# Unread products in TensorE's two pauses of the last stage of a two-layer gated transformer

## The chip, the cores and the metric

The kernel runs on one core of one Trainium2 chip. The metric is the device time of one launch in microseconds. The other engines of the core are named as in the profile: PE is TensorE's matmul, PEld its weight load, DVE is VectorE, ACT is ScalarE, POOL is GpSimd and SP is SyncE.

## The reference

The input x has 8 batches of 256 tokens of 256 features, and ctx has the same shape. Two layers follow each other. Each adds a gated attention and a gated feed-forward part to x:

```python
x = x + tanh(g_xattn[0]) * L0_xattn(layernorm(x), ctx)      # 16 heads of 16
x = x + tanh(g_ffn[0])   * L0_ffn(layernorm(x))             # 64 slots, top 8, a GRU
x = x + tanh(g_xattn[1]) * L1_xattn(ctx, layernorm(x))      # 8 heads of 128
x = x + tanh(g_ffn[1])   * L1_ffn(layernorm(x))
```

The change lies in the last of these four. L1_ffn works on values that are rounded to 8-bit steps:

```python
def _act_fake_quant(x, clip_factor):
    scale = sigmoid(clip_factor) * max(abs(x)) / 127.0       # over the whole tensor
    return clip(round(x / scale), -128, 127) * scale

xq   = _act_fake_quant(x, clip_x)
gate = xq @ quant(w_gate).T          # 256 -> 704
up   = xq @ quant(w_up).T
h    = _act_fake_quant(silu(gate) * up, clip_down)
out  = h @ quant(w_down).T           # 704 -> 256
```

What matters here is that each scale is one maximum over all tokens. No up product can start before the maximum of the whole normed x is known, and no down product before the maximum of the whole h is known. So TensorE has two pauses in this stage.

## The kernel before, in words

Layers 0 and 1 are worked through batch by batch in one long, interleaved run. In `attention1` the loop is over 8 batches of 8 heads, and the pieces of layer 0 for later batches stand in a queue `side` with a cost for each and due times; they are drawn in between the steps of layer 1. When the last batch begins, the queue has been emptied, and `ffn_weights` adds the quantizing and turning of the weights w_gate, w_up and w_down to it. The results are wgT, wuT and wdT, bf16 tiles with 128 partitions. wdT has six blocks of 256 columns.

The last batch ends with `project(0)` and `project(1)` (line 1092, 8 heads each, fp32), then `norm` (the layer norm xl, line 245, and the largest value of the batch, amax, line 1122), then `turn_x` (four transposes of xl, line 254, copied by ACT at line 1129).

The last stage then goes:

1. `act_scale` (lines 1350 to 1363) for x. DVE takes the maximum over the columns of amax (1353), PE transposes the column into a row (1355), DVE takes the maximum of the row (1356), PE spreads the one number over 128 partitions with a product of ones (1358), and DVE makes the scale sx (1360) and its reciprocal rx (1362).
2. `quantize_tokens` (1383) for each batch: a scaling to int8 (1370 on ACT, 1372 on DVE) and a cast to bf16 (1373). The result is xqT.
3. `expand` (1387) for each of four groups of 512 tokens. In each, six tiles of the 704 middle features follow: four products of 128x512 bf16 into a PSUM tile `big` of which there are three (1394), Silu on ACT into sg (1402), and the multiplication into h, on DVE (1409) or for every third tile on ACT and POOL (1406, 1407). `largest` (1427) collects the maxima of h on DVE into hmax.
4. `act_scale` again for h: sh and rh.
5. For each batch, h is scaled and cast to bf16 hq (1370, 1372, 1373), twelve products of 128x256 bf16 go into a PSUM tile `one` (1459), DVE multiplies with the scales into y (1467), POOL adds x (1469, on DVE for the last batch), and SP stores y (1470).

The tiles `one` (two buffers) serve both `act_scale` and the down products. Before the pools `big` and `one` are opened, PSUM is held by the pools of `bank`: four buffers "m", three "z" and one "s".

The order on each engine is set by a scheduler that follows the order in which the kernel was written, except where an instruction is ready sooner. `tc.issue_after(ins)` queues what is written in its block behind `ins` on the same engine; it adds an order and no wait for `ins` to finish.

## Time and profile before

| | us |
|---|---|
| median of 3 timed runs | 1047.76 |
| lowest and highest of them | 1046.73, 1048.28 |
| the profiled execution | 1043.28 |
| its span, first to last instruction | 1041.5 |
| PE busy | 990.5 (95%) |
| DVE busy | 623.7 (60%) |
| ACT busy | 463.9 (45%) |
| POOL busy | 121.5 (12%) |
| mean granted clock of PE | 0.975 |

The stage that the change touches is the last 70 us of the span. It can be read from the timeline:

| from the span's start, us | what |
|---|---|
| 970.87 to 974.59 | the second output projection (1092) on PE |
| 974.59 to 978.17 | PE pauses |
| 978.17 to 980.76 | four transposes of xl, and the two small steps of the first scale on PE |
| 980.76 to 983.14 | PE pauses |
| 983.14 to 1010.88 | up products (1394) |
| 1010.88 to 1014.62 | PE pauses |
| 1014.62 to 1015.94 | the two small steps of the second scale |
| 1015.94 to 1018.35 | PE pauses |
| 1018.35 to 1036.75 | down products (1459) |
| 1038.27 | DVE's last instruction; the last store follows |

The profile gives each engine's busy time by slices and, in the row PEclk, the share of full speed that the clock of the PE array was granted. Views by window give the same numbers for any stretch. In the timeline an instruction's row ends with the idle time of its engine ahead of it and who ended it.

### The profile page before, as it was taken

The page shows a single profiled execution, that of the slowest core. Times are in us where ns is not written, and L with a number is a line of the kernel's source. Part 1 is how long each engine was busy: PE and PEld are TensorE (multiplying, and loading weights), DVE is VectorE, ACT ScalarE, POOL GpSimd, SP SyncE. Part 2 cuts the span into 40 slices and gives each one's busy share as a digit, 9 for nine tenths or more (in the row PEclk, how much of TensorE's full clock was granted, in tenths as well). Part 3 has the DMA queues.
Part 4 walks back from the last instruction along what each step waited for, and adds up shares of the span by engine and source line. Part 5 has one row for each costly group of instructions (what it writes and reads, how often), then busy time and mean ns, then how long its engine had stood idle before and what let it go on. Part 6 is the DMA issues. An engine that isn't in the chain of part 4 may idle for free.

```text
span 1041.5 us, 13065 instructions
## 1 busy us (share of the span) xinstructions
PE 990.5 (95%) x4803; PEld 683.5 (66%) x4803; DVE 623.7 (60%) x1613; ACT 463.9 (45%) x878; POOL 121.5 (12%) x158
## 2 busy tenths in 40 slices
PE   5998799999999999999999999999999999999776
PEld 4765466667677667777776676676776776776423
DVE  5655566656465655756566564566765365454397
ACT  3666335444435533444534434444334234234474
POOL 5201120101010010111001000010000000000134
PEclk9989889999999999999999999999999999999897
DMA  7702200021110101111000100001000000000002
GB/s 172 200 1 72 91 21 21 28 74 41 52 50 22 51 31 41 36 46 41 21 21 31 51 21 21 29 1 56 1 1 1 1 0 1 1 1 1 1 0 82
DMA packets 33536, 37.32 MB, mean 36 GB/s; under 512 B 10368, under 2 KB 28992, under 8 KB 33472
## 3 DMA queue, kind: packets, MB, share of 16 engines
q1 hardware_dynamic: 33472, 36.48, 11.9%
q8 instruction: 38, 0.62, 0.2%
q14 instruction: 26, 0.21, 0.1%
HBM read 28.08 MB, written 8.39 MB: 35 GB/s over the span
## 4 chain that ended last, share of the span: by engine, by line
PE 87%; DVE 7%; ACT 2%; DMA 2%; issue 1%; POOL 1%; SPq 0%; DVEq 0%; ACTq 0%; POOLq 0%
PE bank_m L1020 11%; PE bank_m L1051 11%; PE bank_m L1079 10%; PE bank_m L1033 10%; PE bank_m L1005 6%; PE bank_m L1065 5%; PE bank_m L1092 5%; PE bank_z L598 4%; PE bank_z L635 3%; PE bank_z L622 3%; PE bank_z L506 2%; PE bank_z L535 1%; PE bank_s L845 1%; PE bank_z L671 1%; PE bank_m L254 1%; PE bank_m L635 1%
## 5 line engine op out<-in xcount | busy, mean ns | idle before, releaser
L1053 ACT ACTIVATE e<-bank_m,nm 128x512 f32<-128x512 f32 x128 | 88.0, 688 | 146.2 <-DVE nm L1052 144.0
L1051 PE MATMUL bank_m<-k,q 128*128 128x512 f32 x256 | 127.3, 602 | 0.0
L1020 PE MATMUL bank_m<-kvT,w1kv 128*128 128x512 f32 x256 | 126.1, 604 | 0.0
L1079 PE MATMUL bank_m<-eT,v 128*128 128x256 f32 x512 | 124.8, 381 | 1.1 <-ACT e L1053 0.7
L1079 PEld LDWEIGHTS bank_m<-eT,v 128*128 128x128 f32 x512 | 95.3, 190 | 34.4 <-issue 16.3
L1033 PE MATMUL bank_m<-w1kv,kvT 128*128 128x256 f32 x512 | 116.6, 380 | 0.0
L1052 DVE TENSOR_REDUCE nm<-bank_m 128x1 f32<-128x512 f32 x128 | 87.9, 688 | 33.7 <-PE bank_m L1051 32.9
L1033 PEld LDWEIGHTS bank_m<-w1kv,kvT 128*128 128x128 f32 x512 | 95.9, 190 | 13.7 <-issue 1.1
L625 ACT ACTIVATE e<-bank_z 128x512 f32<-128x512 f32 x112 | 63.2, 596 | 80.9 <-PE bank_z L622 80.7
L240 POOL TENSOR_TENSOR rstd<-rstd,mhalf 128x2 f32<-128x2 f32 x48 | 34.7, 726 | 446.6 <-DVE rstd L239 410.1
L1014 DVE TENSOR_SCALAR q<-bank_m,bq 128x256 f32<-128x256 f32 x64 | 28.1, 479 | 97.1 <-PE bank_m L1005 97.0
L601 DVE TENSOR_REDUCE nf<-bank_z 128x2 f32<-128x512 f32 x112 | 75.0, 683 | 18.0 <-PE bank_z L598 17.6
L1040 DVE COPY v<-bank_m 128x512 f32<-128x512 f32 x64 | 43.9, 686 | 58.0 <-PE bank_m L1033 58.0
L1065 PEld LDWEIGHTS bank_m<-ident,e 128*128 128x128 f32 x512 | 58.5, 140 | 23.4 <-issue 18.2
L1065 PE MATMUL bank_m<-ident,e 128*128 128x128 f32 x512 | 71.4, 275 | 0.4 <-DVE v L1040 0.4
L1022 ACT ACTIVATE k<-bank_m,bk 128x512 f32<-128x512 f32 x64 | 44.0, 688 | 55.2 <-PE bank_m L1020 55.1
L1086 ACT ACTIVATE oT<-bank_m,bv 128x256 f32<-128x256 f32 x64 | 30.3, 474 | 84.4 <-PE bank_m L1079 84.1
L1005 PE MATMUL bank_m<-kvT,w1q 128*128 128x256 f32 x256 | 64.1, 388 | 1.3 <-DVE kvT L991 1.0
L1055 DVE TENSOR_SCALAR e<-e,rs 128x512 f32<-128x512 f32 x128 | 62.1, 485 | 2.2
L1051 PEld LDWEIGHTS bank_m<-k,q 128*128 128x128 f32 x256 | 44.5, 190 | 26.6 <-issue 22.0
L1020 PEld LDWEIGHTS bank_m<-kvT,w1kv 128*128 128x128 f32 x256 | 43.0, 190 | 28.1 <-issue 24.6
L1092 PE MATMUL bank_m<-w1o,oT 128*128 128x256 f32 x256 | 59.6, 380 | 0.6 <-DVE x L1106 0.6
(345 smaller groups left out, 1547.8 us busy)
## 6 DMA issues: line engine op xcount, KB each, us to landing
qs<-dqb SPq DMA_DIRECT2D x96, 64.0 KB, 2.5
ks<-dkb SPq DMA_DIRECT2D x48, 128.0 KB, 2.7
c<-in_ctx_dram SPq DMA_DIRECT2D x8, 256.0 KB, 3.2
x<-in_x_dram SPq DMA_DIRECT2D x8, 256.0 KB, 2.9
w1kv<-in_L_xattn_Wkv_dram SPq DMA_DIRECT2D x4, 512.0 KB, 6.8
out_dram<-y SPq DMA_DIRECT2D x8, 256.0 KB, 2.1
dqb<-hi SPq DMA_DIRECT2D x6, 256.0 KB, 2.1
dqb<-lo SPq DMA_DIRECT2D x6, 256.0 KB, 2.4
```

Of the source, the lines that this page charges most:

```text
L601: V.tensor_reduce(full[:, 2 * half : 2 * half + 2], ps, AX.X, ALU.max, negate=True)
L625: A.activation(e[:, i, :, :], ps, AF.Exp)
L1005: T.matmul(pq[:, i, :], w1q[:, c, h * P : (h + 1) * P], self.kvT[:, c, S:], start=c == 0, stop=c == 1,)
L1020: T.matmul(pk, w1kv[:, c, h * P : (h + 1) * P], self.kvT[:, c, :], start=c == 0, stop=c == 1)
L1033: T.matmul(pv[:, k, :], self.kvT[:, c, kc * P : (kc + 1) * P], w1kv[:, c, at : at + 2 * P], start=c == 0, stop=c == 1,)
L1051: T.matmul(ps, self.q[h][:, qc * P : (qc + 1) * P], self.k[h], start=True, stop=True)
L1052: V.tensor_reduce(nm[:, at], ps, AX.X, ALU.max, negate=True)
L1053: A.activation(e[:, qc, :], ps, AF.Exp, bias=nm[:, at], accum_out=sums[:, at])
L1055: V.tensor_scalar(e[:, qc, :], e[:, qc, :], rs[:, at], None, ALU.mult)
L1065: T.transpose(pt[:, k, qc * P : (qc + 1) * P], self.e[h][:, qc, kc * P : (kc + 1) * P], ident)
L1079: T.matmul(po, self.v[h // 2][:, kc, (h % 2) * P : (h % 2 + 1) * P], self.eT[:, kc, :], start=kc == 0, stop=kc == 3,)
L1092: T.matmul(self.pp[:, qc, :], self.oT[:, h, qc * P : (qc + 1) * P], w1o[:, h, :], start=h == 0, stop=h == H1 - 1,)
```

## The change

A function `keep_busy(to, n)` makes n products of wdT with itself: the first 128 columns are the weights, the first 512 columns are moved through, and the result goes into a PSUM tile that nobody reads. It is called in four places, with 14, 8, 15 and 9 products: behind the second output projection of the last batch, behind the broadcast of the first scale, behind the last up product, and behind the broadcast of the second scale. `project` and `expand` now hand on their last matmul, so that the calls can be queued behind it.

```diff
+WARM = (14, 8, 15, 9)
...
-                T.matmul(
+                self.projected = T.matmul(
                     self.pp[:, qc, :],
                     self.oT[:, h, qc * P : (qc + 1) * P],
                     w1o[:, h, :],
                     start=h == 0,
                     stop=h == H1 - 1,
-                )
+                ).ins
...
+    def keep_busy(to, n):
+
+        w = ffn["wdT"].rearrange("p i d -> p (i d)")[:, :512]
+        for _ in range(n):
+            T.matmul(to, w[:, :P], w, start=True, stop=True)
...
         me.project(0)
         me.project(1)
+        with tc.issue_after(me.projected):
+            keep_busy(bank("s"), WARM[0])
         me.norm()
         me.turn_x()
...
-        def act_scale(maxima, clip_col, name):
+        def act_scale(maxima, clip_col, name, after):
...
-            T.matmul(pb[:, 0:1], ones[:1, :], m[:1, 1:2], start=True, stop=True)
+            bc = T.matmul(pb[:, 0:1], ones[:1, :], m[:1, 1:2], start=True, stop=True)
+            with tc.issue_after(bc.ins):
+                keep_busy(one(), after)
...
-        sx, rx = act_scale(amax, clip[:, 0:1], "x")
+        sx, rx = act_scale(amax, clip[:, 0:1], "x", WARM[1])
...
-        expand(NB - 1)
+        filled = expand(NB - 1)
         while hold:
             largest()
 
-        sh, rh = act_scale(hmax, clip[:, 1:2], "h")
+        with tc.issue_after(filled):
+            keep_busy(one(), WARM[2])
+        sh, rh = act_scale(hmax, clip[:, 1:2], "h", WARM[3])
```

Nothing that the reference asks for is left out or computed in another way.

More of the change, by code (lines that the diff above doesn't have):

```diff
@@ L1393, in expand @@
                     for c in range(2):
-                        T.matmul(
+                        ins = T.matmul(
                             pg[:m, w, :],
@@ L1399, in expand @@
                             stop=c == 1,
-                        )
+                        ).ins
                 sg = fp.tile([P, 512], F32, tag="sg", name="sg", bufs=3)
@@ L1420, in expand @@
                     hold.append((3 * n + 2, n, 5 if last else 3, 6))
+            return ins
         hold = []
```

## The prediction

> **What bounds the kernel now.** I read the slices first. TensorE (PE) is busy nearly everywhere, but its busy share falls in the last three slices, and there the granted clock falls too.

> ```profile
> PE   5998799999999999999999999999999999999776
> ...
> PEclk9989889999999999999999999999999999999897
> ```

> So I asked for the busy time in windows. The clock changes at 976.80, 987.04, 1014.35 and 1024.59 us; the distances 10.24, 27.31 and 10.24 are 3, 8 and 3 times 3.413, so I cut on that grid. After the stretch come its length, then busy us (instructions) of PE, PEld, DVE, ACT and POOL, then the granted clock, DMA share and GB/s. The first two rows are from early in the kernel.

> ```profile
> 27.89:31.31 3.42, 2.21 (x15) 1.46 (x14) 3.34 (x11) 1.18 (x3) 0.34 (x1) 1.00 0.76 249
> 92.75:96.16 3.41, 2.21 (x15) 1.76 (x16) 2.59 (x7) 2.49 (x5) 1.91 (x3) 1.00 0.81 200
> 973.39:976.80 3.41, 1.20 (x6) 0.72 (x4) 1.70 (x6) 0.00 (x0) 0.29 (x1) 1.00 0.00 0
> 976.80:980.21 3.41, 1.60 (x6) 0.83 (x6) 1.75 (x7) 0.58 (x1) 2.13 (x5) 0.50 0.00 0
> 983.63:987.04 3.41, 3.41 (x10) 1.21 (x9) 0.00 (x0) 2.76 (x6) 0.65 (x1) 0.50 0.00 0
> 987.04:990.45 3.41, 3.41 (x17) 1.30 (x15) 2.53 (x3) 2.78 (x6) 0.98 (x2) 1.00 0.02 5
> 1010.93:1014.35 3.42, 0.00 (x0) 0.00 (x0) 3.42 (x5) 0.68 (x1) 0.27 (x1) 1.00 0.00 0
> 1014.35:1017.76 3.41, 0.95 (x3) 0.57 (x3) 2.17 (x9) 1.33 (x2) 0.00 (x0) 0.50 0.00 0
> 1017.76:1021.17 3.41, 2.38 (x10) 1.02 (x11) 3.25 (x5) 3.41 (x4) 0.00 (x0) 0.50 0.00 0
> 1021.17:1024.59 3.42, 3.42 (x15) 1.45 (x13) 1.56 (x2) 3.42 (x3) 1.73 (x1) 0.50 0.01 2
> 1028.00:1031.41 3.41, 2.30 (x16) 1.28 (x15) 3.41 (x5) 1.47 (x1) 2.26 (x2) 1.00 0.23 82
> ```

> The reader is to see: after a window with PE busy 1.20 (973.39) or 0.00 (1010.93) the clock halves; it comes back only after a window that is full (983.63, 1021.17); 2.38 busy at half clock (1017.76) did not bring it back. Busy 2.30 at full clock (1028.00) kept it. With 2.21 it was once lost (27.89) and once kept (92.75). I put the bound for keeping near 2.2 of 3.41.

> The timeline shows what the half clock costs.

> ```profile
> 983.14 1.01 PE L1394 MATMUL big<-xqT,wgT 128*128 128x512 bf16 x2 [2.38 <-ACT xqT L1373]
> ...
> 987.64 0.59 PE L1394 MATMUL big<-xqT,wgT 128*128 128x512 bf16 x2
> ...
> 988.76 0.69 ACT L1402 ACTIVATE sg<-big,cg 128x512 f32<-128x512 f32 x1 [0.23 <-PE big L1394]
> ...
> 1022.09 0.69 DVE L1467 TENSOR_TENSOR y<-one,srow 128x512 f32<-128x512 f32 x1 [1.08 <-PE one L1459]
> ...
> 1024.98 0.69 DVE L1467 TENSOR_TENSOR y<-one,srow 128x512 f32<-128x512 f32 x1 [1.33 <-PE one L1459]
> ```

> Two up products take 0.85 us at half clock (starts 984.80 and 985.65) and 0.43 at full (987.64 and 988.07). ScalarE waits for PE before each of its first sg, and VectorE waits 1.08 and 1.33 us for the down products. The chain of waits agrees: 4.68 us of PE at L1394 from 983.14 and 5.34 us of PE at L1459 from 1019.61 end last. Between them VectorE is the bound: from 993.55 to 1014.40 it has no pause over about 0.1 us.

> [...]

> **The change, part by part.** The instruction order shows only PE changed: 46 products with their weight loads. The 14 stand behind the last output projection, 8 behind the first scale's broadcast, 15 behind the last up product, 9 behind the second scale's broadcast. None of them carries a wait. No DMA, ACT, DVE or POOL instruction is moved.

> *The added products.* At full clock one costs 0.216 us: 128x512 bf16, as L1394 at 987.64. What stands behind them on PE waits for other engines anyway:
> - 14 x 0.216 = 3.02 us; PE is idle 3.58 us there (974.59 to 978.17, waiting for xl).
> - 8 x 0.216 = 1.73; idle 2.38 (980.76 to 983.14, for xqT).
> - 15 x 0.216 = 3.24; idle 3.73 (1010.89 to 1014.62, for mh).
> - 9 x 0.216 = 1.94; idle 2.41 (1015.94 to 1018.35, for hq).

> The least slack is 0.47, so I cost them at nothing. At half clock they are 5.98, 3.42, 6.40 and 3.84 and overshoot by 2.4, 1.0, 2.7 and 1.4: that is the price if the cover is gone.

> *The added waits.* PE waits for its own earlier products at the second scale's transpose and before batch 1's down products (WAW on a `one` bank): long done, nothing. Three more allocations turn the two `one` banks: batch 0's down product takes the bank that sh reads at 1015.98, free 2 us before 1018.35. Nothing.

> *First gap.* With the clock held, the three transposes from 978.71 to L1355 (0.67 us) take half, -0.34. L1355 at 0.42 comes near the 0.27 of L611's full-clock median, -0.1; L1358 at 0.58 near 0.42 (L367: 0.17 to 0.25 each), -0.15. So xqT and all behind it come 0.6 earlier. PE then starts up products at 982.5, and a tile of four takes 0.86 instead of 1.71. Tile 0 is ready at 983.6, before ScalarE has done its casts (984.83 - 0.6 = 984.2). From there ScalarE runs back to back at about 0.6 each: sg0 984.2, up0 984.8, sg1 985.4, sg2 986.0, sg3 986.6 instead of 988.76, 2.2 earlier. VectorE: h1 at 986.1 instead of 987.47, h2 986.8, the first hmax 987.65 instead of 989.42: 1.8 earlier. What is late next is VectorE itself; h4 stands behind hmax, so the 1.8 goes on to 1014.4.
> Will the clock hold? PE is busy until 977.65, then only about 1.0 to 1.3 us until the 8 start at 980.1. The worst window, 977.65 to 981.06, has 1.6 to 2.1: under my bound. So it may fall between about 979.8 and 981.7. Then up to 8 products run at 0.43 and the up products start near 983.6 instead of 982.5, but the window is full and the clock is back by then or one window later: tile 0 at 984.6, gain 1.4. Ends: 0.6 (clock back late) and 2.2. I take 1.8.

> *Second gap.* L1355 and L1358 cost -0.2. The worst windows hold about 2.0 to 2.4 busy, at the bound or over it. With the clock held, down products start-to-start are 0.145 us (12 in 1.78, at 1029.13) instead of 0.25. Batch 0's last nine, from 1019.57, are done at 1021.05: y0 at 1021.1 instead of 1022.09, -1.0. Batch 1's twelve follow until 1022.65: y1 at 1022.8 instead of 1024.98, -2.15. Behind it VectorE is continuous to 1035.6, and what it needs from ScalarE is there (the cast of batch 3 ends at 1023.87, before qh of batch 6 would start at 1024.3), so -2.15 reaches the end; the last PE wait of 1.25 us stays, since that batch waits for y5's bank. Ends: 0 (clock lost) and 2.6 (both waits and the small steps); I take 2.15 + 0.2 = 2.3.

> **Sum.** 1.8 + 2.3 = 4.1 us against the profiled execution: 1043.28 us, of which 1041.5 is span. The median of the timed runs, 1047.76, lies 4.48 above it; I take the difference over. [...] So 4.4: 1047.76 - 4.4 = 1043.4 us.

> **The rivals.**
> - One gap only. The window around the short groups of down products has about 2.0 busy and may lose the clock. For: 2.21 lost it once. Against: 2.30 kept it. Then 1.8 + 0.3 remain, about 1045.6.
> - Full clock, but ScalarE takes over. It is busy 4.79 to 5.00 us of each 5 from 990 to 1000; if its queue does not start earlier, the first gap is worth 0.6 only: 1047.76 - 0.6 - 2.3 = 1044.9. Against: its waits before sg name PE.
> - It doesn't do what it says: the products don't keep the clock, or it falls in the same places; delay and earlier return cancel: 1047.8.
> - Slower. The products run at half clock and stand in front of the real ones. Place: PE's queue at 974.6, 980.8, 1010.9 and 1015.9; price up to 7.5 us, with nothing gained: 1055.3. It decides if the clock is already down, or falls, while one of the longer groups runs: a product at half clock takes 0.21 more, so more than two of the 15 (slack 0.49) already hold up mh. Against: the windows before both gaps are busy 2.84 and 2.95 and at full clock.

> **How the numbers follow.** Forecast 0.60, own range 1041.6 to 1044.9; one gap 0.17; ScalarE 0.10; no effect 0.08; slower 0.05. The range reaches over the first three to 1046.0 and leaves the last two and the ends out. About 0.2%, 2.1 us, can be told from no change. Faster by more: 0.60 + half of 0.17 + 0.09 = 0.78; within: 0.17; slower: 0.05.

> **What would show it.** In the changed profile: PE clock 1.00 in the windows from 983 to 988 and from 1015 to 1024, or a short dip near 980; up products 0.43 for two from the first tile; the first sg not waiting for PE; the waits of 1.08 and 1.33 us before y gone; the added products ended before xl, xqT, mh and hq arrive. Wrong if the last stage keeps a half clock behind 1018, if L254 or L1355 wait for the added products, or if the first hmax is less than 1 us earlier relative to the last projection.

## The result and the profile after

The changed kernel takes 1040.92 us in the median of 9 runs (1038.1 to 1043.36), the kernel before 1046.73 in the median of 9 (1043.22 to 1050.4). The medians lie 5.8 us apart. The recorded ratio of the two kernels, which I go by, is 0.9958 with a 95% interval of 0.9943 to 0.9974: 4.4 us less, between 2.7 and 6.0. The profiled execution has a span of 1040.2 us.

The slices of the profile, in the same two rows as before: the last three slices are now at full clock.

```profile
PE   5999899999999999999999999999999999999886
...
PEclk9988889999999999999999999999999999999999
```

The view by windows on the clock's grid; columns as in the prediction. In this trace too the clock changes on a grid of 3.413 us: its half-clock spells ahead of the stage last 10.24, 10.24, 6.83 and 6.83 us. The grid stands at another place than in the profile before.

```profile
976.03:979.45 3.42, 3.42 (x18) 2.00 (x17) 1.70 (x6) 0.00 (x0) 0.13 (x1) 1.00 0.00 0
979.45:982.86 3.41, 2.26 (x13) 1.06 (x11) 1.75 (x7) 0.58 (x1) 2.48 (x5) 1.00 0.00 0
982.86:986.27 3.41, 2.86 (x14) 1.26 (x14) 1.89 (x7) 2.86 (x5) 0.41 (x2) 1.00 0.03 7
1010.17:1013.58 3.41, 3.41 (x17) 1.30 (x15) 3.31 (x5) 1.79 (x3) 1.30 (x1) 1.00 0.00 0
1013.58:1016.99 3.41, 2.55 (x13) 1.12 (x12) 2.38 (x6) 0.00 (x1) 0.00 (x0) 1.00 0.00 0
1016.99:1020.41 3.42, 2.30 (x13) 0.81 (x10) 3.42 (x6) 3.42 (x4) 0.00 (x0) 1.00 0.02 5
```

Every window is granted the full clock. The two weakest hold 2.26 and 2.30 us of PE work, just over the 2.21 behind which the clock was once lost and once kept in the kernel before. No other place of the grid would have been weaker by more than 0.01: slid over the two pauses, a stretch of 3.41 us holds at least 2.26 and 2.29 us of PE work.

The timeline after, on DVE, ACT, PE and POOL. The line numbers are those of the changed file: 1251 the added products, 1406 the up products, 1414 sg, 1474 the down products, 1482 y.

```profile
977.24 3.19 PE L1251 MATMUL bank_s<-wdT 128*128 128x512 bf16 x14
...
985.30 0.59 PE L1406 MATMUL big<-xqT,wgT 128*128 128x512 bf16 x2 [0.55 <-ACT xqT L1385]
...
986.90 0.68 ACT L1414 ACTIVATE sg<-big,cg 128x512 f32<-128x512 f32 x1
...
989.55 0.69 ACT L1414 ACTIVATE sg<-big,cg 128x512 f32<-128x512 f32 x1 [0.25 <-POOL h L1419]
...
1021.67 0.69 DVE L1482 TENSOR_TENSOR y<-one,srow 128x512 f32<-128x512 f32 x1
...
1022.44 3.85 POOL L1484 TENSOR_TENSOR y<-y,x 128x512 f32<-128x512 f32 x2 [10.48 <-DVE y L1482]
...
1023.40 0.69 DVE L1482 TENSOR_TENSOR y<-one,srow 128x512 f32<-128x512 f32 x1 [0.17 <-PE one L1474]
1024.01 1.16 DVE L1385 CAST hq<-qh 128x1536 bf16<-128x1536 int8 x1
```

The up products start at full speed (starts 985.30 and 985.73, 0.43 us for two). The first sg no longer waits for PE; the fourth (989.55) waits for POOL instead. Of the two waits of 1.08 and 1.33 us before y, 0.17 is left.

To compare profiles I count from one event, the start of VectorE's second update of x by the last projection (974.63 in the profile before, 977.45 after), because the time up to there differs between profiles of equal code by up to 5 us. "mh" is the start of the reduction behind the last hmax, "end" the end of VectorE's last instruction. In us:

| kernel | first hmax | mh | mh to end | whole stage | ratio to before (95%) |
|---|---|---|---|---|---|
| before | 14.79 | 39.77 | 23.87 | 63.64 | |
| after | 12.82 | 37.72 | 21.75 | 59.47 | 0.9958 (0.9943 to 0.9974) |
| again | 12.82 | 37.72 | 21.74 | 59.46 | 0.9942 (0.9925 to 0.9959) |
| gap1 | 12.82 | 37.75 | 23.25 | 61.00 | 0.9982 (0.9959 to 1.0005) |
| gap2 | 14.82 | 39.78 | 21.66 | 61.44 | 0.9968 (0.9956 to 0.9981) |
| thin | 14.79 | 39.77 | 23.87 | 63.64 | 0.9989 (0.9976 to 1.0003) |
| half | 12.84 | 37.77 | 23.09 | 60.86 | 0.9973 (0.9946 to 1.0000) |
| over | 13.88 | 38.24 | 23.05 | 61.29 | 0.9965 (0.9951 to 0.9979) |
| short_only | 13.70 | 38.63 | 21.84 | 60.47 | 0.9970 (0.9954 to 0.9985) |
| long_only | 14.47 | 39.44 | 23.68 | 63.12 | 0.9985 (0.9970 to 1.0000) |
| rows32 | 14.85 | 39.82 | 24.84 | 64.66 | 1.0020 (1.0005 to 1.0036) |
| cols32 | 12.82 | 37.74 | 21.76 | 59.50 | 0.9946 (0.9931 to 0.9962) |
| early1 | 12.82 | 37.42 | 21.77 | 59.19 | 0.9952 (0.9937 to 0.9968) |
| early2 | 12.83 | 37.75 | 21.74 | 59.49 | 0.9952 (0.9937 to 0.9968) |

The stage is 4.17 us shorter: 2.05 up to mh, 2.12 behind it.

### The profile page after: what moved, and what is told of

Its sections match the earlier page's. It is cut to its first block, busy times and chain, and to the rows that moved or that the text cites. A ratio compares the mean times of both kernels' runs of the same rounds, so it can differ in the third digit from the quotient of the medians.

```text
span 1040.2 us, 13158 instructions
## 1 busy us (share of the span) xinstructions
PE 999.1 (96%) x4849; PEld 688.4 (66%) x4849; DVE 624.2 (60%) x1613; ACT 463.0 (45%) x878; POOL 121.1 (12%) x158
## 4 chain that ended last, share of the span: by engine, by line
PE 87%; DVE 7%; ACT 3%; issue 1%; POOL 1%; DMA 1%; SPq 0%; DVEq 0%; ACTq 0%; POOLq 0%
PE bank_m L1022 11%; PE bank_m L1053 11%; PE bank_m L1081 10%; PE bank_m L1035 10%; PE bank_m L1007 6%; PE bank_m L1067 5%; PE bank_m L1094 5%; PE bank_z L600 4%; PE bank_z L624 3%; PE bank_z L637 3%; PE bank_z L508 3%; PE bank_z L537 1%; PE bank_s L847 1%; PE bank_z L673 1%; PE bank_m L256 1%; PE bank_m L637 1%
```

## The experiments

My theory: the products keep PE busy enough in each window that the clock stays, and that alone makes the real products of this stage faster. Rivals: the changed order or turn of the PSUM tiles made the gain; only both pauses together pay; any busy PE will do; the products themselves delay the real work.

### Each pause alone: gap1 and gap2

```diff
-WARM = (14, 8, 15, 9)
+WARM = (14, 8, 0, 0)      # gap1
+WARM = (0, 0, 15, 9)      # gap2
```

A call with no products is left out, with its tile.

> Only the first two groups (14 and 8 products). If the gain is the held clock in each pause by itself: from the last batch's second update of x to the start of the reduction mh 37.7 us as after the change (39.8 before), from there to VectorE's last instruction 23.2 as before; 2.0 us faster than before, ratio about 0.998. If the gain came from the second pause alone: no change. If the added work only pays in both together: under 1 us.

> Only the last two groups (15 and 9 products). If each pause pays by itself: 39.8 us from the second update of x to mh as before, 21.1 from there to VectorE's end (23.2 before); about 2.1 us faster, ratio about 0.998. If the second pause holds the clock only when the first did: no change.

(These two, and the two runs behind them, count the stage to the start of VectorE's last instruction; the table counts to its end, 0.69 us later.)

gap1 reached mh at 37.75 and gap2 needed 21.66 behind it: each pause pays by itself, with the sizes expected. The two gains do not wait for each other. One number is off: gap1's second half, with no products in it, took 23.25 instead of 23.87. In gap1 the clock fell 1.5 us before mh and was back 8.75 us behind it, in the kernel before it fell with mh and was back 10.2 us behind it. The whole first half is 2.0 us earlier against the grid, so the half clock meets another part of the work; this explanation was not tested by itself. The ratios agree with this, but gap1's interval reaches 1.

### The same places without work: thin

```diff
-            T.matmul(to, w[:, :P], w, start=True, stop=True)
+            T.matmul(to[:32, :1], w[:, :32], w[:, :1], start=True, stop=True)
```

> All 46 products, in the same places and into the same tiles, but with 32 columns of weights and 1 column moved, so that they keep PE busy for a small part of the time. If the clock is what counts: it halves in both pauses, 63.0 us from the second update of x to VectorE's end as before, ratio 1.000. If the changed order or the other turn of the PSUM tiles brought the gain: 58.8 us, ratio 0.996. The results of the real computation are not changed.

PE's timeline of this kernel: the first group now is over in half a microsecond, and the four transposes behind it take 1.42 us again, as at half clock in the kernel before (0.30 and 0.55 us after the change).

```profile
976.27 0.50 PE L1251 MATMUL bank_s<-wdT 128*32 128x1 bf16 x14
979.92 1.42 PE L256 MATMUL bank_m<-ident,xl 128*128 128x128 f32 x4 [3.15 <-DVE amax L1124]
```

Every mark of the stage is that of the kernel before to 0.01 us. Order, waits and tiles are those of the changed kernel, so these bring nothing; the gain comes from the work that PE does there (stage 63.64 us without it, 59.47 with it).

### Once more: again

No edit; the changed kernel.

> The changed kernel once more, to see it at another place of the clock's windows. If the products hold the clock at any place: 58.8 us from the second update of x to VectorE's end, within 0.5, and ratio 0.996. If they hold it only at some places: a half clock at about 980 or 1019 in this profile, and up to 2 us longer.

59.46 us. The clock held with the grid 0.9 us later against the stage than in the first profile. early2 below, with the same pauses, has the grid 1.6 us later than the first profile, and its stage takes 59.49.

### Fewer products: half

```diff
-WARM = (14, 8, 15, 9)
+WARM = (7, 4, 8, 5)
```

> Half of the products: 7, 4, 8 and 5. The stretches between groups grow by 1.5, 0.9, 1.5 and 0.9 us. If a window keeps the clock only from about 2.2 us busy on, it falls in both pauses: first hmax about 14.2 us after the second update of x (12.8 with all products, 14.8 with none), whole stage about 62.5 us (59.5 and 63.6). If a little activity is enough: 59.5.

The windows of this kernel at both pauses:

```profile
977.49:980.90 3.41, 1.41 (x8) 0.91 (x9) 1.78 (x8) 0.59 (x1) 2.49 (x5) 1.00 0.00 0
980.90:984.32 3.42, 2.75 (x7) 0.81 (x6) 1.85 (x7) 3.00 (x6) 0.28 (x2) 0.50 0.02 7
1011.62:1015.04 3.42, 1.23 (x6) 0.68 (x7) 2.39 (x7) 0.10 (x1) 0.00 (x0) 1.00 0.00 0
1015.04:1018.45 3.41, 2.21 (x8) 0.56 (x6) 3.41 (x6) 3.41 (x4) 0.00 (x0) 0.50 0.00 0
```

The clock fell in both pauses, behind windows with 1.41 and 1.23, as expected. But 2.75 in one window was enough to bring it back at 984.32, so the first hmax came at 12.84, not at 14.2, and the stage at 60.86, not at 62.5: my expectation took a wholly busy window as the condition, and that was wrong. The first pause could do with half of the products, at this place of the grid. In the second pause 2.21 did not bring it back, and of the 2.12 us only 0.78 are left.

### Too many products: over

```diff
-WARM = (14, 8, 15, 9)
+WARM = (22, 14, 24, 15)
```

> More than fits: 22, 14, 24 and 15 products, at 0.216 us 4.75, 3.02, 5.18 and 3.24 us for pauses of 3.58, 2.38, 3.73 and 2.41. The clock holds, and the overshoot stands on the path: the transposes of xl 1.2 later, the up products 1.0 to 1.6 later in all, the transpose of mh another 1.45, the last group nothing or 0.1, since ScalarE's half of batch 0 comes later. Stage about 62 to 62.6 us instead of 59.5. If PE's queue let the real work go ahead of the products: 59.5.

PE's timeline of this kernel at the first pause:

```profile
974.59 4.70 PE L1251 MATMUL bank_s<-wdT 128*128 128x512 bf16 x21
979.12 0.60 PE L256 MATMUL bank_m<-ident,xl 128*128 128x128 f32 x4
```

(One of the 22 products has no record here.) The transposes start 4.55 us behind the update of x instead of 3.54: they wait for the products. The stage takes 61.29 us, a little less than the 62 to 62.6 expected. The up products were 1.1 us later and the first hmax still 1.06, but mh only 0.5: ScalarE did a cast (0.5 us) ahead of its first sg that in the changed kernel stands behind its fourth, and VectorE has one wait of 0.42 less before mh. Behind mh 1.30 was lost, where the estimate was 1.45. So the price of the products that did not fit was here the overshoot, less what the engines behind made up again.

### One group of each pair: short_only and long_only

```diff
-WARM = (14, 8, 15, 9)
+WARM = (0, 8, 0, 9)       # short_only
+WARM = (14, 0, 15, 0)     # long_only
```

> Only the short groups (8 and 9), behind each scale's broadcast. The clock is lost in the long pauses, and the short groups run at half speed, 3.4 and 3.8 us, past the end of their pauses by about 1.0 and 1.4. But they fill the window before the real products, so the clock comes back one window earlier: first hmax about 13.8 us after the second update of x (14.8 before, 12.8 with all), stage 61 to 62 us. If an earlier return doesn't help or the overshoot decides: 63.6 or more.

> Only the long groups (14 and 15). The small steps of both scales run at full clock (0.66 and 0.2 us gained), but the short pauses stay empty, with about 1 us busy in a window, so the clock falls just before or within the first real products: first hmax 13.5 to 14.5 us after the second update of x, stage 61.5 to 63. If the long groups alone are enough: 59.5.

The windows of short_only (first two rows) and of long_only:

```profile
981.81:985.22 3.41, 3.08 (x8) 1.47 (x10) 1.89 (x7) 2.40 (x5) 0.57 (x2) 0.50 0.01 2
1015.94:1019.35 3.41, 3.08 (x9) 1.25 (x10) 3.17 (x8) 2.78 (x3) 0.00 (x0) 0.50 0.00 0
```

```profile
976.44:979.85 3.41, 2.11 (x11) 0.96 (x9) 1.85 (x8) 0.59 (x1) 2.48 (x5) 1.00 0.00 0
1017.39:1020.80 3.41, 2.94 (x12) 1.11 (x12) 2.60 (x3) 3.41 (x4) 0.00 (x0) 0.50 0.02 5
```

The 17 short products gave 3.17 of the 4.17 us, the 29 long ones 0.52; the stages, 60.47 and 63.12, lie 0.5 below and 0.1 above what was expected. In short_only the clock is lost in both pauses, but the products in front of the real ones fill a window at half clock (3.08) and bring it back before the first up product (985.44) and before the down products (from 1019.60). In long_only the clock holds through the small steps and then falls, at 979.85 behind 2.11 and at 1017.39 behind 0.63, so that the real products pay the whole return. So in these two profiles it is the place right before the real work that counts most.

### Over 32 rows, over 32 columns: rows32 and cols32

```diff
-            T.matmul(to, w[:, :P], w, start=True, stop=True)
+            T.matmul(to, w[:32, :P], w[:32, :], start=True, stop=True)     # rows32
+            T.matmul(to[:32, :], w[:, :32], w, start=True, stop=True)      # cols32
```

> All 46 products at full length, but over 32 rows of the array instead of 128. If time in which PE streams is what holds the clock: stage 59.5 us from the second update of x to VectorE's end, as with the changed kernel. If the share of the array that works counts: the clock falls in both pauses, 63.6 us, as in the kernel before. The full early window of products over 64 and 72 rows, behind which the clock fell, speaks for the second. The results of the real computation are not changed.

> All 46 products at full length and over 128 rows, but with 32 columns of weights, so a quarter of the array's width. If streaming time or rows count: 59.5 us for the stage. If columns count as well: 63.6.

A window of rows32 with the 15 products behind the up products, and the next one:

```profile
1012.22:1015.63 3.41, 3.33 (x15) 1.24 (x15) 3.41 (x5) 0.68 (x1) 0.31 (x1) 1.00 0.00 0
1015.63:1019.05 3.42, 2.63 (x8) 1.21 (x9) 2.09 (x8) 1.19 (x2) 0.00 (x0) 0.50 0.02 5
```

PE was busy 3.33 of 3.41 us, and the clock was lost. With 32 columns instead it held all the same, and the stage took 59.50. The window of the small steps in the first pause, of rows32 and then of cols32, is the closest pair:

```profile
978.09:981.50 3.41, 2.36 (x14) 1.06 (x12) 1.83 (x8) 0.59 (x1) 2.49 (x5) 1.00 0.00 0
976.25:979.66 3.41, 2.36 (x13) 1.12 (x12) 1.79 (x8) 0.58 (x1) 2.49 (x5) 1.00 0.00 0
```

PE is busy for the same 2.36 us; behind the first the clock fell, behind the second it stayed. So here products over 32 of the 128 rows did not hold the clock, and products over 32 of the 128 columns did. The kernel before agrees: early in it the clock fell behind a window with 3.32 us of products over 64 and 72 rows (62.03 to 65.44). rows32 also shows what the slower rival describes: its second group in the second pause runs at half clock in front of the real products (from 1015.63 on, clock 0.50), the stage takes 64.66, and the kernel is slower than before, by 0.05 to 0.36%.

### Products in earlier pauses: early1 and early2

```diff
+EARLY = {(1, 3, 1): (8, "m")}                     # early1
+EARLY = {(1, 3, 1): (8, "m"), (2, 0, 1): (6, "s")} # early2
...
+    def fill_early(n, tag):
+        to = bank(tag)
+        for _ in range(n):
+            T.matmul(to[:, :P], ones, ident, start=True, stop=True)
...
+                n = EARLY.get((self.b, g, half))
+                if n and i == 0:
+                    with tc.issue_after(ins):
+                        fill_early(*n)
```

> The changed kernel, and 8 fp32 products of 128x128 (1.7 us) at another place: batch 1's last half of exponentials in layer 0, where PE waits 1.85 us for VectorE and the clock then falls for two windows, 6.8 us, in both kernels. If these windows are bound by PE: up to 3.4 us earlier at the end of layer 1, ratio to the kernel before about 0.993. If VectorE or DMA bounds them, or the next window drops the clock anyway: 0.996.

> As the previous one, and 6 more such products in batch 2's first group, where PE waits 1.49 us. The scheduler moves a few of layer 1's projections ahead of that group's products. Up to 3.4 us more if both spells go: ratio about 0.990; 0.993 to 0.996 if one stays; above that if the moved projections delay batch 2.

PE's timeline of early1: the products stand in the pause (the 8 fp32 products are 16 instructions).

```profile
115.39 1.95 PE L450 MATMUL bank_m<-ident,ones 128*128 128x128 f32 x16
117.24 0.50 PE L630 MATMUL bank_z<-qs,ks 72*128 72x256 f32 x2
```

The clock no longer fell there (granted clock 1.00 from 106 to 133; in the kernel before it is at half from 116.64 to 123.47). But early1's profile has 8 windows at half clock ahead of the last stage, early2's 6, and the others between 8 and 11, the kernel before 8 too. The ratios of both, 0.9952, lie among those of the changed kernel (0.9942 to 0.9958). A further gain is not shown; these runs leave it open.

## Why the prediction was right

**The bound for keeping the clock** (near 2.2 us of 3.41). It served, but it is not a bound. In the pauses it fits: kept with 2.26 and 2.30 after, lost with 2.11 in long_only. Elsewhere, with 128 rows too, it doesn't: short_only kept the clock behind 2.00 (1009.11, up products), and the changed kernel behind 1.68 early on (16.88, fp32 products). With 32 rows it was lost behind 2.36. So PE's busy time alone doesn't decide, and that the pauses needed 2.2 is not shown. What I wrote as the condition for the return, a full window, was too strict: 2.75 in half and 3.08 in short_only did it. Nor is it always enough: 2.94 in long_only did not do it, and in rows32 not even a window that down products filled wholly (1022.46 to 1025.87). Where the lines lie stays open. That the gain comes with the held clock does not hang on this: the stage takes 63.64 in thin and 64.66 in rows32, which lost it, and 59.50 in cols32, which held it.

**The added products cost nothing.** Right. 14 of them ran from 977.24 to 980.43, the transposes then waited 0.56 us for VectorE; behind the other three groups PE waited 0.55, 0.49 and 0.36. over shows the price when there are too many (stage 61.29), rows32 when the clock is lost (64.66).

**First gap, 1.8.** It gave 2.05. The small steps gave 0.66 (0.6 forecast): the first up product stands 7.85 us behind the update of x instead of 8.51. The fourth sg came 2.03 earlier instead of 2.2, since it met a wait that I had not seen: its buffer is read by POOL's h, 0.25 us. The fall of the clock that I allowed for at about 979.8 to 981.7 did not come. My worst window, 1.6 to 2.1, was summed too low: by the figures beside it (1.0 to 1.3 until 980.1, then 0.96 of the 8 products) it is 2.0 to 2.3, and it measured 2.26. The 1.8 was a middle value between a fall and none, so that it came near is in part luck. In half the clock did fall, at 980.90, and it cost next to nothing, as I had allowed for: the window behind held 2.75 us of work, and the clock was back at 984.32.

**Second gap, 2.3.** It gave 2.12: the small steps 0.21 (0.2 forecast), and y1 another 2.14 (2.15 forecast), but of this only 1.91 reached the end. The difference is the term for what stands behind y1: the cast of hq that took 0.95 us before takes 1.16, while POOL's two additions now run back to back, 3.85 us, and meet within it. In the eight profiles where they do, this cast takes 1.16 to 1.17; in the other six, where a single addition begins just behind the cast's start, 0.95. That POOL is the cause was not tested by itself. I had taken VectorE's queue behind y1 as moved unchanged.

**Sum.** 4.1 forecast against the profiled execution, 4.17 in the stage; the errors of the two terms, 0.25 and -0.18, cancel in part. The forecast time, 1043.4, lies 2.5 us above the 1040.92 measured, and that lies below the forecast's own range (1041.6 to 1044.9). 1.0 of that is the start: it was counted from 1047.76, the median of three runs, and nine have 1046.73. The rest, 1.4, is the gap between the difference of the medians and the 4.4 of the ratio. The 0.3 in the step from 4.1 to 4.4 was my guess at what the kernel before loses more, on average, when its clock comes back at another place than in the profile; no trace showed it, and the profiles do not support it. In the twelve whose early code is the same, the last update of x lies 833.4 to 834.3 us behind the clock's last early return. So in these profiles the pauses are met at places of the grid that lie within 0.9 us. Whether that also holds in timed runs is not shown; their interval, 2.7 to 6.0, does not tell 4.1 from 4.4.

**The rivals.** One gap only: fell, both hold. ScalarE takes over: fell, the first hmax came 1.97 earlier. No effect: fell with thin. Slower: rows32 shows it (stage 64.66), but with products that did not hold the clock; those of the change did.

## What to carry to other kernels

Where TensorE's real work starts behind a short pause, look at the granted clock there, window by window, before looking for a faster order; a filler just ahead of the real products paid most here (3.17 of the 4.17 us), and one over 32 of the array's 128 rows did not hold the clock (lost behind 3.33 us of 3.41). Count its length at the full clock (0.216 us a product here) against the pause: in over, the transposes waited for it, 4.55 us behind the update of x instead of 3.54. Compare such edits by a stage within the profile: here it repeated to 0.04 us (after, again, cols32 and early2), where the timed runs of the changed kernel spread over 5.
